# An S4 convolution and a Strassen FFN on one core: the first phase by pairs of row blocks

## The chip, the core and the metric

The kernel runs on one core of a Trainium2 chip. The metric is the device time in microseconds of one execution, the median of three runs. TensorE is PE (its weight loads PEld), VectorE DVE, ScalarE ACT, GpSimd POOL; SP is the engine whose queue issues nearly all transfers.

## What is computed

`x` has 4 batches of 1024 rows of 2048, float32: 32 row blocks of 128 rows, eight of one batch.

```python
mod = (silu(c) @ wmod).reshape(4, 6, 1, 2048)        # six sections, per batch
sa, ca, ga, sb, cb, gb = (mod[:, i] for i in range(6))
ga, gb = (sign(g) * max(abs(g), 0.25) for g in (ga, gb))
h = layernorm(x) * (1 + ca) + sa
x = x + ga * (causal_conv(h, K) + D * h)             # K: one S4 filter of 2048 taps, from Lambda, p, q, B, Ct, step
h = layernorm(x) * (1 + cb) + sb
x = x + gb * (h @ W.T + bias + low_rank_update(h))   # 16 adapters of rank 16, weighted sum
```

The convolution runs along the 2048 elements of a row, so it is a product with one triangular Toeplitz matrix of 2048 x 2048.

## The kernel before

Start. The filter is worked out (`s4`, `toeplitz`) and laid out as three 128-row tables `kf[f]`, each as a float16 high and low part. At the same time the sections 1 and 0 of the modulation (`ca`, `sa`) are formed: 16 steps each, a step loads 1 MB of `wmod` (`mod_load`, L312) and runs its matmuls (`mod_mm`, L317). `X0` says at which steps the first two blocks of x are loaded.

First phase, row block by row block (`r` from 0 to 31). `stats` (L493) takes mean and variance, `normalize` (L508) writes (x - mean) * rstd to a tile `n` on DVE. `conv_prep` (L522) works in four pieces of four 128-column chunks: four transposes on PE into PSUM (L535), four ACT instructions with scale `ca` and bias `sa` into `t` (L538), sums of neighbouring chunks (`sm`, L544), and the split of chunks and sums into a float16 high part (ACT copy, L546) and a low part (DVE subtraction, L547). `conv_mm` (L550) makes a row block's product in two halves `q`, each from three families of matmuls (L567); a family multiplies high by high, high by low and low by high. Family 0 works on the sums; ACT copies its result to `qs` (L580); family 2 gives the odd chunks with `qs` (L584), family 1 adds to family 0's PSUM and gives the even ones. The gate is multiplied in (L586, L593) and x is added with a running sum (L594). `conv_post` (L607) stores `y` to a scratch tensor `x1d`, takes the variance by an ACT Square that writes its elements over x, and keeps mean and rstd for the second layer norm in `ln2`.

Blocks 0 and 1 start before their gate is known (section 2 is formed meanwhile): `conv_late` (L598) gates them afterwards.

Between matmuls stand the generator `tick` and a list `PLAN`, one string for each of the 10 ticks of a row block: S is a step of fill, N a piece of the next block's preparation, T the statistics of the block after it, F its normalizing, P the block before's `conv_post`, L a step of the second phase's `left`. Fill (`rest`, L863) starts at block R0 = 3: it prepares the low-rank factors (`prep_lora`, L380), merges them into W in eight rounds (`merge`, L424, matmuls `lps` L443) and stores the merged weights as float16 pairs to `wcd`; every second step is one of sections 4, 3 and 5 of the modulation. The order on each engine is fixed when the program is built; it is mainly the text's, with single instructions pulled ahead where their operands are free.

Second phase. `left` (L636) loads two blocks of `x1d`, normalizes, transposes, modulates (256 wide, L655) and builds the seven left operands of a Strassen product, which it stores to `lfd` and keeps; `ffn_unit` (L692) multiplies them with the seven weights (L703), adds gate and bias to the residual (L721 to L728) and stores. It runs over all 16 units for the first half of the output columns and again for the second. The weights are loaded in `ORDER` = 0, 4, 5, 1, 6, 2, 3: weight 0 has a pool of its own, the next two (`XW`) reuse the four x tiles, the rest the space that the first phase leaves.

Of the kernel before, what the change touches and what calls it, by code (L numbers as in the profile page):

```python
# [34 lines left out]
class Net:  # L35
# [28 lines left out]
    def rstd(self, pool, var, out, n, name, scale=1.0):  # L64

        v = self.nc.vector
        ve = pool.tile([P, n], F32, tag=name + "_v", name=name + "_v")
        t = pool.tile([P, n], F32, tag=name + "_t", name=name + "_t")
        v.tensor_scalar(ve, var, 0.25 * scale, 0.25e-5, MUL, ADD)
        self.nc.scalar.activation(t, ve, AF.Sqrt)  # L70
        v.reciprocal(out, t)
        v.scalar_tensor_tensor(t, ve, out, t, MUL, ADD)
        v.reciprocal(out, t)

# [263 lines left out]
    def mod_gate(self, pool, name, bias=None):  # L338
# [10 lines left out]
        if bias is not None:  # L349
            bt = pool.tile([P, 512], F32, tag="mg2", name="mg2")  # L350
            for q in range(4):
                nc.sync.dma_start(out=bt[32 * q : 32 * q + 32], in_=bias[ds(512 * q, 512)].partition_broadcast(32))
            v.tensor_tensor(bt, bt, g, MUL)
            outs.append(bt)
# [138 lines left out]
    def stats(self, pl, x, tag):  # L493
        v = self.nc.vector
        st = pl["sm"].tile([P, 4, 6], F32, tag="st" + tag, name="st" + tag)
        for q in range(4):
            v.bn_stats(st[:, q], x[:, ds(512 * q, 512)])  # L497
        mv = pl["sm"].tile([P, 2], F32, tag="mv" + tag, name="mv" + tag)
        v.bn_aggr(mv, st)
        rs = pl["sm"].tile([P, 1], F32, tag="rs" + tag, name="rs" + tag)  # L500
        self.rstd(pl["sm"], mv[:, 1:2], rs, 1, "r" + tag)
        if tag in ACTNORM:
            mb = pl["sm"].tile([P, 1], F32, tag="mb" + tag, name="mb" + tag)
            v.scalar_tensor_tensor(mb, mv[:, 0:1], -1.0, rs, MUL, MUL)
            return mb, rs
        return mv, rs

    def normalize(self, pl, x, st, tag):  # L508
        n = pl["n"].tile([P, D], F32, tag="n", name="n" + tag)
        m, rs = st  # L510
        if tag in ACTNORM:
            self.nc.scalar.activation(n, x, AF.Identity, bias=m, scale=rs)
        else:
            self.nc.vector.tensor_scalar(n, x, m[:, 0:1], rs, SUB, MUL)
        return n

    def conv_load(self, pl, r):
        x = pl["x"].tile([P, D], F32, tag=f"x{r % 4}", name="x")
        self.nc.sync.dma_start(out=x, in_=self.io["x"][ds(P * r, P), :])
        return x  # L520

    def conv_prep(self, pl, r, x, st, out):  # L522
        nc, v = self.nc, self.nc.vector
        b = r // 8
        n = self.normalize(pl, x, st, "1")
        yield

        hc = [pl["h"].tile([P, NC, P], F16, tag=f"hc{x}", name=f"hc{x}") for x in range(2)]
        hs = [pl["h"].tile([P, HC, P], F16, tag=f"hs{x}", name=f"hs{x}") for x in range(2)]
        out[r] = hc, hs  # L530
        for c0 in range(0, NC, 4):
            tp = self.tps.tile([P, 4, P], F32, tag="t", name="tp")
            t = pl["t"].tile([P, 4, P], F32, tag="t", name="t")
            for k in range(4):
                nc.tensor.transpose(tp[:, k], n[:, ds(P * (c0 + k), P)], self.ident)  # L535
            for k in range(4):
                c = c0 + k
                nc.scalar.activation(  # L538
                    t[:, k], tp[:, k], AF.Identity,
                    bias=self.sa[:, c, b : b + 1], scale=self.ca[:, c, b : b + 1],  # L540
                )
            tv = t.rearrange("p (i e) n -> p i e n", e=2)
            sm = pl["t"].tile([P, 2, P], F32, tag="sm", name="sm")
            v.tensor_tensor(sm, tv[:, :, 0, :], tv[:, :, 1, :], ADD)  # L544
            for (hi, lo), src, sl in ((hc, t, slice(c0, c0 + 4)), (hs, sm, slice(c0 // 2, c0 // 2 + 2))):
                nc.scalar.copy(hi[:, sl], src)  # L546
                v.tensor_tensor(lo[:, sl], src, hi[:, sl], SUB)  # L547
            yield

    def conv_mm(self, pl, hs, x, tick, early):  # L550
        nc, v = self.nc, self.nc.vector
        hc, hs = hs
        y = pl["y"].tile([P, D], F32, tag="y", name="y")
        yv = y.rearrange("p (j e t) -> p j e t", e=2, t=P)
        if not early:
            gv = self.gat.rearrange("p (j e t) -> p j e t", e=2, t=P)
        sums = pl["sm"].tile([P, 2], F32, tag="sums", name="sums")

        def family(ps, f, q, first):
            pf = ps.rearrange("p j t -> p (j t)")  # L560
            last = 4 * q + 3
            for i in range(last + 1):
                o = P * max(0, i - 4 * q)
                k0 = P * max(0, 4 * q - i)
                for x, z in ((0, 0), (0, 1), (1, 0)):
                    h = hs[x][:, i] if f == 0 else hc[x][:, 2 * i + 2 - f]
                    nc.tensor.matmul(  # L567
                        pf[:, o:512], h, self.kf[f][z][:, ds(k0, 512 - o)],
# [6 lines left out]
        for q in range(2):  # L575
            jj = slice(4 * q, 4 * q + 4)
            pa = self.acc.tile([P, 4, P], F32, tag="a", name="ya")
            family(pa, 0, q, True)
            qs = pl["t"].tile([P, 4, P], F32, tag="qs", name="qs")
            nc.scalar.copy(qs, pa)  # L580
            tick()
            pb = self.acc.tile([P, 4, P], F32, tag="a", name="yb")
            family(pb, 2, q, True)
            v.tensor_tensor(yv[:, jj, 1, :], pb, qs, ADD)  # L584
            if not early:
                v.tensor_tensor(yv[:, jj, 1, :], yv[:, jj, 1, :], gv[:, jj, 1, :], MUL)  # L586
            tick()
            family(pa, 1, q, False)
            sl = ds(1024 * q, 1024)
            if early:  # L590
                nc.scalar.copy(yv[:, jj, 0, :], pa)
            else:
                v.tensor_tensor(yv[:, jj, 0, :], pa, gv[:, jj, 0, :], MUL)  # L593
                v.scalar_tensor_tensor(y[:, sl], y[:, sl], 1.0, x[:, sl], MUL, ADD, accum_out=sums[:, q : q + 1])  # L594
            tick()
        return y, sums

    def conv_late(self, x, y, sums):  # L598

        v = self.nc.vector  # L600
        for q in range(2):
            sl = ds(1024 * q, 1024)
            v.tensor_tensor(y[:, sl], y[:, sl], self.gat[:, sl], MUL)
            v.scalar_tensor_tensor(y[:, sl], y[:, sl], 1.0, x[:, sl], MUL, ADD, accum_out=sums[:, q : q + 1])
# [87 lines left out]
    def ffn_unit(self, pl, u, q, lf, wc, tick):  # L692
# [25 lines left out]
        for r, h in ((0, 0), (1, 1), (0, 1), (1, 0)):  # L718
            x = pl["o"].tile([P, 512], F32, tag="o", name="xo")
            nc.sync.dma_start(out=x, in_=at(self.x1d[2 * u : 2 * u + 2].rearrange("r p d -> (r p) d"), r, h))  # L720
            v.tensor_tensor(x, x, self.gbias[:, h], ADD)  # L721
# [39 lines left out]
ACTNORM = ""  # L761

MR = 2
ACC, TPS = 5, 2
PLAN = ("PNSL", "NL", "NSL", "NTL", "SL", "SL", "SL", "SL", "FSL", "SSL")
LPLAN = ("LL", "LL", "LL", "LL", "L", "0", "")
R0 = 3
WM, WMS = 3, 3
X0 = (21, 27)
LEFT0 = 30  # L770
# [12 lines left out]
def net(ctx: ExitStack, tc: tile.TileContext, io):  # L783
# [5 lines left out]
    k.ln2 = k.const("ln2", [P, 32, 2])  # L789
    k.lfd = k.dram.tile([NU, 7, P, HC, 2, P], F16, tag="lfd", name="lfd")  # L790
# [55 lines left out]
    xs, hs = {}, {}  # L846
    sts = {}
    n = 0
    for sec in (1, 0):
        for _ in section(sec, (wms, wmp)):  # L850
# [3 lines left out]
            if n in X0:  # L854
                r = X0.index(n)
                xs[r] = k.conv_load(pl, r)
                sts[r] = k.stats(pl, xs[r], "1")
            n += 1
    xs[2] = k.conv_load(pl, 2)
    st.close()  # L860
    for name, bufs in (("h", 2), ("n", 1), ("t", 2), ("y", 2), ("g", 1)):
# [19 lines left out]
    XW = {ORDER[1]: (0, 1), ORDER[2]: (2, 3)}  # L881

    def load_w(q, i):

        wc[i] = []
        for j in range(2):
            if i in XW:
                w = pl["x"].tile([P, D], F32, tag=f"x{XW[i][j]}", name=f"w{i}").bitcast(F16)
            else:
                w = pr["w" if i == ORDER[0] else "v"].tile([P, 2 * D], F16, tag=f"w{i}{j}", name=f"w{i}")  # L890
# [4 lines left out]
    def early():  # L895
        right.close()
        for name, bufs in (("w", 1), ("l", 8), ("t", 1), ("s", 1), ("x2", 1)):
            pr[name] = pool(p2, "p2" + name, bufs, "right")
        load_w(0, ORDER[0])
# [7 lines left out]
    def step():  # L907
        if r >= R0 and "w" not in pr and next(fill, 0) == 0:
            early()

    def prep(r):
        return k.conv_prep(pl, r, xs[r], sts.pop(r), hs)

    def load(r):
        xs[r] = k.conv_load(pl, r)

    def stats(r):
        sts[r] = k.stats(pl, xs[r], "1")

    sec = section(2, (wmp,))  # L920
    take(prep(0), 9)
    take(prep(1), 9)
    stats(2)
    take(sec, 16)
    load(3)
    ys = {0: k.conv_mm(pl, hs.pop(0), xs[0], lambda: None, True)}
    take(prep(2), 9)
    stats(3)
    ys[1] = k.conv_mm(pl, hs.pop(1), xs[1], lambda: None, True)
    nxt = prep(3)  # L930
    take(nxt, 1)
    take(sec, 1)
    k.gat = k.gate_tile(pl["g"], 0)
    for r in range(2):
        k.conv_late(xs[r], *ys[r])
        k.conv_post(pl, r, xs.pop(r), *ys[r])
    post = None
    for r in range(2, 32):
        if r + 2 < 32:
            load(r + 2)  # L940
        if r % 8 == 0:
            k.gat = k.gate_tile(pl["g"], r // 8)
        if r == 31:
            load_w(0, ORDER[1])
        if r == LEFT0:
            while "w" not in pr:
                step()
            lgen = next_left(0)
        plan = iter(PLAN)
        follow = []  # L950

        def tick():
            for a in next(plan):
                if a == "S":
                    step()
                elif a == "P" and post:
# [109 lines left out]
```

## Time and profile before

| | us |
|---|---|
| median of three runs | 2149.41 (2148.75 to 2149.71) |
| the profiled execution, its own time | 2148.25 |
| its span, first to last instruction | 2146.5 |
| busy PE, DVE, ACT, POOL | 2077.2, 1322.7, 926.2, 3.4 |
| first conv matmul, last one | 110.4, 924.8 |
| second phase's first matmul | 924.9 |

The mean granted clock of PE is 0.982; 483 MB are moved. A busy PE is no PE at its peak, since ends of matmuls are modelled: in the second phase matmuls of 512 columns start every 0.216 us and are shown as 0.379 each. The profile's lines of groups give the tile names, shapes and count, then busy time and mean, then the idle time of that engine before them with what ended it.

### The profile page before, as it was taken

The page shows a single profiled execution, that of the slowest core. Times are in us where ns is not written, and L with a number is a line of the kernel's source. Part 1 is how long each engine was busy: PE and PEld are TensorE (multiplying, and loading weights), DVE is VectorE, ACT ScalarE, POOL GpSimd, SP SyncE. Part 2 cuts the span into 40 slices and gives each one's busy share as a digit, 9 for nine tenths or more (in the row PEclk, how much of TensorE's full clock was granted, in tenths as well). Part 3 has the DMA queues.
Part 4 walks back from the last instruction along what each step waited for, and adds up shares of the span by engine and source line. Part 5 has one row for each costly group of instructions (what it writes and reads, how often), then busy time and mean ns, then how long its engine had stood idle before and what let it go on. Part 6 is the DMA issues. An engine that isn't in the chain of part 4 may idle for free.

```text
span 2146.5 us, 28399 instructions
## 1 busy us (share of the span) xinstructions
PE 2077.2 (97%) x11084; PEld 1021.9 (48%) x11084; DVE 1322.7 (62%) x2357; ACT 926.2 (43%) x1699; POOL 3.4 (0%) x12
## 2 busy tenths in 40 slices
PE   5698999999999999999999999999999999999998
PEld 1244545455455555654545545545444444444444
DVE  6549789988999998666565566565433323332323
ACT  1057667766677776655554455455200000000000
POOL 0000000000000000000000000000000000000000
PEclk8699999999999999999999999999999999999999
DMA  9988477767874553387465565565795545554542
GB/s 397 371 289 319 160 299 282 287 251 277 313 299 181 185 208 118 114 347 280 170 245 194 178 233 198 193 240 181 267 353 168 186 153 168 168 165 165 174 159 70
DMA packets 127137, 483.06 MB, mean 225 GB/s; under 512 B 13670, under 2 KB 13799, under 8 KB 96023
## 3 DMA queue, kind: packets, MB, share of 16 engines
q1 hardware_dynamic: 126464, 479.65, 61.7%
q8 instruction: 87, 1.43, 0.3%
q10 hardware_dynamic: 538, 1.59, 0.2%
q14 instruction: 48, 0.39, 0.1%
HBM read 325.89 MB, written 155.30 MB: 224 GB/s over the span
## 4 chain that ended last, share of the span: by engine, by line
PE 75%; DVE 11%; ACT 5%; DMA 2%; issue 1%; SPq 0%; POOL 0%; ACTq 0%; DVEq 0%
PE fZ L703 22%; PE fX L703 15%; PE fY L703 15%; PE ya L567 10%; PE yb L567 5%; PE tp L653 3%; PE lps L443 2%; PE modps L317 2%; ACT x L613 1%; PE tp L535 1%; ACT t L538 1%; DVE y L594 1%; DVE st L497 1%; DVE hc L547 1%; DVE wch L471 1%
## 5 line engine op out<-in xcount | busy, mean ns | idle before, releaser
L703 PEld LDWEIGHTS <-lf 128*128 128x128 f16 x5376 | 525.9, 98 | 620.8 <-issue 1.1
L703 PE MATMUL fZ<-w,lf 128*128 128x512 f16 x2304 | 513.6, 379 | 0.8 <-ACT p L711 0.8
L703 PE MATMUL fX<-w,lf 128*128 128x512 f16 x1536 | 342.8, 379 | 0.0
L703 PE MATMUL fY<-w,lf 128*128 128x512 f16 x1536 | 342.0, 379 | 0.0
L567 PEld LDWEIGHTS <-hc 128*128 128x128 f16 x2304 | 214.5, 98 | 202.0 <-issue 39.3
L721 DVE TENSOR_TENSOR xo<-xo,gb 128x512 f32<-128x512 f32 x128 | 87.8, 690 | 242.0 <-DMA xo<-x1d 229.6
L538 ACT ACTIVATE t<-tp,sa,ca 128x128 f32<-128x128 f32 x512 | 201.3, 473 | 13.2 <-DVE sa L376 5.1
L567 PE MATMUL ya<-kh,hs 128*128 128x512 f16 (+3 forms) x768 | 194.5, 328 | 0.7 <-DVE hs L547 0.7
L567 PE MATMUL ya<-kh,hc 128*128 128x512 f16 (+3 forms) x768 | 191.5, 327 | 3.2 <-ACT qs L580 3.2
L567 PE MATMUL yb<-kh,hc 128*128 128x512 f16 (+3 forms) x768 | 191.1, 326 | 0.0
L711 ACT COPY p<-fZ 128x512 f32<-128x512 f32 x64 | 37.2, 582 | 285.9 <-PE fZ L703 272.1
L711 ACT COPY p<-fX 128x512 f32<-128x512 f32 x32 | 18.7, 586 | 316.0 <-PE fX L703 240.9
L567 PEld LDWEIGHTS <-hs 128*128 128x128 f16 x1152 | 107.7, 98 | 98.4 <-issue 20.0
L655 ACT ACTIVATE gt<-tp,sb,cb 128x256 f32<-128x256 f32 x256 | 124.9, 575 | 60.9 <-PE tp L653 60.9
L317 PE MATMUL modps<-wm,sct 128*32 128x512 f32 x768 | 120.0, 687 | 28.4 <-DMA wm<-in_wmod 19.8
L567 PE MATMUL ya<-kl,hs 128*128 128x512 f16 (+3 forms) x384 | 126.1, 328 | 0.0
L567 PE MATMUL ya<-kl,hc 128*128 128x512 f16 (+3 forms) x384 | 125.5, 327 | 0.0
L567 PE MATMUL yb<-kl,hc 128*128 128x512 f16 (+3 forms) x384 | 125.4, 326 | 0.0
L726 DVE TENSOR_TENSOR fin<-fX,gb 128x512 f32<-128x512 f32 x32 | 22.1, 692 | 128.0 <-PE fX L703 127.9
L535 PE MATMUL tp<-ident,n 128*128 128x128 f32 x512 | 80.6, 282 | 15.1 <-ACT t L538 11.8
L547 DVE TENSOR_TENSOR hc<-t,hc 128x512 f16<-128x512 f32 x128 | 87.5, 683 | 5.5 <-ACT hc L546 5.5
L443 PE MATMUL lps<-lbh,lac 128*128 128x512 f16 x256 | 85.6, 382 | 1.3 <-ACT lbh L418 0.8
(241 smaller groups left out, 2212.8 us busy)
## 6 DMA issues: line engine op xcount, KB each, us to landing
wm<-in_wmod SPq DMA_DIRECT2D x96, 1024.0 KB, 6.3
lfd<-lf SPq DMA_DIRECT2D x112, 512.0 KB, 3.3
lf<-lfd SPq DMA_DIRECT2D x112, 512.0 KB, 3.9
x<-in_x SPq DMA_DIRECT2D x32, 1024.0 KB, 5.2
x1d<-y SPq DMA_DIRECT2D x32, 1024.0 KB, 5.7
x<-x1d SPq DMA_DIRECT2D x32, 1024.0 KB, 5.3
xo<-x1d SPq DMA_DIRECT2D x128, 256.0 KB, 3.9
out<-xo SPq DMA_DIRECT2D x128, 256.0 KB, 3.6
```

The costliest lines, as they stand in the source:

```text
L317: self.last = self.nc.tensor.matmul(self.modps[32 * g : 32 * g + 32, :], self.sct[:, j].rearrange("p r b -> p (r b)"), w[:, ds(512 * g, 512)],
L443: nc.tensor.matmul(ps, la[:, x, k, h], y[:, k, osl], start=(n == 0), stop=(n == 5))
L535: nc.tensor.transpose(tp[:, k], n[:, ds(P * (c0 + k), P)], self.ident)
L538: nc.scalar.activation(t[:, k], tp[:, k], AF.Identity, bias=self.sa[:, c, b : b + 1], scale=self.ca[:, c, b : b + 1],)
L547: v.tensor_tensor(lo[:, sl], src, hi[:, sl], SUB)
L567: nc.tensor.matmul(pf[:, o:512], h, self.kf[f][z][:, ds(k0, 512 - o)], start=first, stop=(i == last and (x, z) == (1, 0)), skip_group_chec ...
L653: nc.tensor.transpose(tp[:, c, r], xs[r][:, ds(P * (c0 + c), P)], self.ident)
L655: nc.scalar.activation(t[:, c0 + c], tp[:, c], AF.Identity, bias=self.sb[:, c0 + c, b : b + 1], scale=self.cb[:, c0 + c, b : b + 1],)
L703: nc.tensor.matmul(ps[name], lf[i][:, k, x, :], wc[i][k // 4][:, k % 4, y, :], start=(first and n == 0), stop=(n == 3 * HC - 1), skip_grou ...
L711: nc.scalar.copy(t, ps[name])
L721: v.tensor_tensor(x, x, self.gbias[:, h], ADD)
L726: v.tensor_tensor(t, cv, self.gbt[:, h], MUL)
```

## The change

The first phase goes by pairs `g` of row blocks. Both blocks' x are loaded together, and the statistics of both are finished together (`rstd` for two columns). Normalizing is an ACT instruction in place, over x itself; the residual is then rebuilt as x * std, without the mean, and the second phase adds the mean (`mv1`) where it adds the bias. A piece of the preparation covers four chunks of both blocks: eight transposes, four ACT instructions of 256, one sum of 512, and one high copy and one low subtraction of 1536 each (chunks and sums in one tile). `conv_mm` makes the first half of block 0, the first half of block 1, then the second halves. PLAN has 18 strings for a pair: O is the last piece of this pair's own preparation, N a piece of the next pair's, T its statistics, P the `conv_post` of the pair before's second block, Q that of this pair's first, S a step of fill and of `left`. Fill starts with pair 1. The tile `n`, the pool `w`, R0 and LEFT0 are gone, `mg2` shares a buffer; weights 0 and 4 take the x tiles.

```diff
-    def normalize(self, pl, x, st, tag):
-        n = pl["n"].tile([P, D], F32, tag="n", name="n" + tag)
...
-            self.nc.vector.tensor_scalar(n, x, m[:, 0:1], rs, SUB, MUL)
+    def stats(self, pl, g, xs):
...
+        rs = pl["sm"].tile([P, 2], F32, tag="rs", name="rs")
+        std = self.rstd(pl["sm"], mv[:, :, 1], rs, 2, "r1")
+        nb = pl["sm"].tile([P, 2], F32, tag="nb", name="nb")
+        v.scalar_tensor_tensor(nb, mv[:, :, 0], -1.0, rs, MUL, MUL)
+        return rs, nb, std
...
+    def conv_prep(self, pl, g, xs, st, out):
...
+        for r in range(2):
+            nc.scalar.activation(xs[r], xs[r], AF.Identity, bias=nb[:, r : r + 1], scale=rs[:, r : r + 1])
+        yield
+        out[g] = []
+        for k in range(4):
+            h = pl["h1" if k == 3 else "h2"].tile([P, 2, 6, 2, P], F16, tag=f"h{k}", name=f"h{k}")
+            t = pl["t"].tile([P, 6, 2, P], F32, tag="t", name="t")
+            out[g].append(h)
+            for i in range(2):
+                tp = self.tps.tile([P, 2, 2, P], F32, tag="t", name="tp")
+                for c in range(2):
+                    for r in range(2):
+                        nc.tensor.transpose(tp[:, c, r], xs[r][:, ds(P * (4 * k + 2 * i + c), P)], self.ident)
+                for c in range(2):
+                    d = 4 * k + 2 * i + c
+                    nc.scalar.activation(
+                        t[:, 2 * i + c], tp[:, c], AF.Identity,
+                        bias=self.sa[:, d, b : b + 1], scale=self.ca[:, d, b : b + 1],
+                    )
+            tv = t[:, 0:4].rearrange("p (i e) r n -> p i e r n", e=2)
+            v.tensor_tensor(t[:, 4:6], tv[:, :, 0], tv[:, :, 1], ADD)
+            nc.scalar.copy(h[:, 0], t)
+            v.tensor_tensor(h[:, 1], t, h[:, 0], SUB)
             yield
...
         for q in range(2):
+            for r in range(2):
+                y = ys[r]
...
+                family(pa, 0, q, r, True)
+                qs = pl["q"].tile([P, 4, P], F32, tag="qs", name="qs")
+                nc.scalar.copy(qs, pa)
+                tick()
...
+    def residual(self, x, y, std, sums, q):
+        sl = ds(1024 * q, 1024)
+        self.nc.vector.scalar_tensor_tensor(
+            y[:, sl], x[:, sl], std, y[:, sl], MUL, ADD, accum_out=sums[:, q : q + 1]
+        )
...
-            v.tensor_tensor(x, x, self.gbias[:, h], ADD)
+            m = self.mv1[:, 2 * u + r, 0:1]
+            v.scalar_tensor_tensor(x, x, m, self.gbias[:, h], ADD, ADD)
...
-PLAN = ("PNSL", "NL", "NSL", "NTL", "SL", "SL", "SL", "SL", "FSL", "SSL")
+PLAN = (
+    "POS", "S", "S", "S", "S", "S",
+    "TS", "S", "NS", "S", "S", "NS",
+    "QS", "NS", "S", "NS", "S", "S",
+)
...
-X0 = (21, 27)
-LEFT0 = 30
+X0 = 22
...
-    for name, bufs in (("h", 2), ("n", 1), ("t", 2), ("y", 2), ("g", 1)):
+    for name, bufs in (("h2", 2), ("h1", 1), ("t", 2), ("q", 1), ("y", 2), ("g", 1)):
...
-    XW = {ORDER[1]: (0, 1), ORDER[2]: (2, 3)}
+    XW = {ORDER[0]: (0, 1), ORDER[1]: (2, 3)}
...
+    for g in range(16):
+        if g:
+            if g + 1 < 16:
+                load(g + 1)
+            if g % 4 == 0:
+                k.gat = k.gate_tile(pl["g"], g // 4)
+        if g == 15:
+            while "l" not in pr:
                 step()
+            load_w(0, ORDER[0])
             lgen = next_left(0)
```

## The prediction

> **What bounds the kernel now.** I read the page's slices first, then a table of windows cut at the stage borders, then the waits of TensorE (PE) inside the first phase, then the groups of instructions with shapes kept apart.
>
> ```profile
> PE   5698999999999999999999999999999999999998
> DVE  6549789988999998666565566565433323332323
> ACT  1057667766677776655554455455200000000000
> PEclk8699999999999999999999999999999999999999
> ```
>
> A slice is 53.7 us. From slice 3 on PE is full to the end. DVE is nearly as full, but only to slice 14, ScalarE (ACT) never. A change that lightens DVE and ACT can therefore pay only where one of them, and not PE's own work, holds PE. The windows ask where that is (columns: window, length, busy time of PE, PEld, DVE, ACT, POOL, granted clock, DMA share, GB/s):
>
> ```profile
> 0.00:107.00 107.00, 68.67 (x326) 20.96 (x326) 62.11 (x165) 10.29 (x17) 1.91 (x10) 0.74 0.95 384
> 165.00:198.00 33.00, 32.05 (x192) 18.09 (x190) 31.32 (x71) 26.18 (x48) 0.00 (x0) 1.00 0.89 332
> 198.00:222.00 24.00, 16.13 (x75) 6.38 (x74) 23.11 (x59) 21.15 (x39) 1.06 (x1) 0.72 0.74 290
> 222.00:724.00 502.00, 494.03 (x3044) 257.33 (x3042) 447.58 (x909) 341.98 (x698) 0.00 (x0) 1.00 0.69 259
> 724.00:800.00 76.00, 72.55 (x454) 41.87 (x452) 73.35 (x167) 63.24 (x135) 0.38 (x1) 1.00 0.56 205
> 800.00:885.00 85.00, 84.17 (x538) 49.91 (x537) 69.62 (x158) 49.32 (x120) 0.00 (x0) 1.00 0.27 100
> ```
>
> Up to 107 us DMA sets the pace (0.95 of it busy: the modulation weights). From 222 to 885 PE idles 7.97 + 3.45 + 0.83 = 12.3 us, 12.6 with 885 to 925 (39.70 of 40). In 800 to 885, where no other work is mixed in, a row block takes 19.66 us (the copies qs at 826.20, 845.87, 865.53), and PE is busy 99% of it: no edit to DVE or ACT can shorten that. The one real hole is 198 to 222; on PE it reads
>
> ```profile
> 202.26 1.09 PE L535 MATMUL tp<-ident,n 128*128 128x128 f32 x8 [1.48 <-DVE n L514]
> 204.61 0.66 PE L535 MATMUL tp<-ident,n 128*128 128x128 f32 x4 [1.25 <-ACT t L538]
> 209.80 1.92 PE L317 MATMUL modps<-wm,sct 128*32 128x512 f32 x2 [1.86 <-DMA wm<-in_wmod]
> 212.53 0.58 PE L443 MATMUL lps<-lbh,lac 128*128 128x512 f16 x1 [0.82 <-ACT lbh L418]
> ```
>
> PE waits for normalizing, for modulation, for a weight tile, and then for the low-rank factors (`lbh`), whose preparation stands among the late gating of blocks 0 and 1 on a full DVE. Work in these 24 us at full rate: 26 modulation matmuls of 0.133, 16 transposes of 0.11, 7 lps and some 20 ya of 0.2: 11 us. So 13 us are lost.
>
> **The change, part by part.** Durations are from these rows:
>
> ```profile
> L538 ACT ACTIVATE t<-tp,sa,ca 128x128 f32<-128x128 f32 x512 | 201.3, 473 | 13.2 <-DVE sa L376 5.1 <-PE tp L535 3.2 <-DVE hc L547 3.1
> L655 ACT ACTIVATE gt<-tp,sb,cb 128x256 f32<-128x256 f32 x256 | 124.9, 575 | 60.9 <-PE tp L653 60.9
> L547 DVE TENSOR_TENSOR hc<-t,hc 128x512 f16<-128x512 f32 x128 | 87.5, 683 | 5.5 <-ACT hc L546 5.5
> L666 DVE TENSOR_TENSOR lf<-gt,lf 128x1024 f16<-128x1024 f32 x64 | 76.7, 1220 | 13.7 <-ACT lf L665 13.6
> L514 DVE TENSOR_SCALAR n<-x,mv,rs 128x2048 f32<-128x2048 f32 x32 | 42.9, 1341 | 4.2 <-PE tp L535 3.6
> L643 ACT ACTIVATE x<-x,ln 128x2048 f32<-128x2048 f32 x32 | 67.1, 2096 | 29.0 <-DMA x<-x1d 29.0
> ```
>
> Modulation: 512 ACT instructions of 128 become 256 of 256 wide, just the shape of L655 in the second phase: 201.3 to 124.9, ACT -76. The fp16 split: per pair of blocks eight copies of 512 and eight of 256 (82.1 + 54.8 us) become four of 1536. Copies of 512, 1024, 2048 take 0.64, 1.05, 1.89, so 1536 takes 1.47; 64 of them 94 us: ACT -43. Its subtraction: 0.683 at 512, 1.22 at 1024, so 1.76 at 1536; 64 are 112 against 87.5 + 53.2: DVE -28. The sums: 64 of 512 wide (44) for 128 of 256 (53.5): DVE -10. Normalizing leaves DVE (-42.9) for ACT, at 2.1 by L643: +67. Small statistics work for two blocks at once: some 1.0 us a pair for 0.68 a block, DVE -6, ACT -3. The residual keeps its form (1.22). Sums: DVE -87, ACT -55, PE nothing: transposes and matmuls keep number and size. In the second phase 128 additions at L721 (0.690) become the three-operand form, 0.744 at L445: DVE +7, hidden, as DVE is busy 324 of 535 us from 1000 to 1535; if uncovered, 7 us.
>
> What of this reaches PE:
> 1. **Idle of 222 to 925.** The windows 400 to 420, 540 to 560, 680 to 700 show DVE at 20.00, 20.00 and 19.70 of 20 and PE idle 2.45, 1.66, 2.75; with 3.45 in 724 to 800 (DVE 73 of 76) 10.3 of the 12.6 us stand where DVE is full. DVE loses 87 us of about 800, 2.2 in 20, so most of it closes: -8 (bounds 0 and -12.6). Next late there: nothing but PE.
> 2. **The hole.** DVE is busy 54.4 of 57 us from 165 to 222, three blocks are handled there, and a block gets 87/32 = 2.7 lighter: 8 us. The chain leaves DVE at 200 for ACT (lb, lbh) and returns at 212.5, so half comes through: -4. Bounds: -13, and +17 by the first rival. The row shows the granted clock at 0.72, and ya starting every 0.43 us from 212.9 to 218 that start every 0.22 later. The Trainium skill ("TensorE: Matmul & The Clock Gate", Part 1) says that the clock halves after an idle window of about 3.4 us and comes back after as long a busy one. By the row, shortening the hole by 4 is worth 4; by the rule the half-speed stretch (about 3.5 us of my 13) goes only if no idle window is left. I keep the row's: the hole does not close.
> 3. **The start.** Both x of pair 0 are loaded at step 22, and pair 1 is loaded before the end of the weight stream: one more MB in a saturated DMA, 2.5 us at 400 GB/s. The first usable split comes after 4 modulations (2.1), a sum (0.7) and a copy of 1.47 instead of 0.64: about +1. But both blocks' first halves follow at once, and the section-2 matmuls fill. Normalizing (4.2 on ACT, busy 10 of 107 us) is covered by the wait for `sa`. I take +2 (0 to +4).
> 4. **The opening of the second phase.** Weight 0 moves into x0 and x1, freed by pair 14 and so loaded in time; weight 4 now takes x2 and x3, and x3 is freed only by the last Square (929.2 to 931.1). So 11 MB instead of 9 follow that point (2.45 us each), one half of weight 4 first, whose matmuls start at 930.9 and need it 2.6 us later: +2 (-1 to +5). Left(0) gets 10 steps in one pair instead of two blocks, so its seven stores on SP no longer stand in front of the weights: that is the -1.
> 5. **New waits.** Load g+1 of x stands on SP behind the Square of the pair before: about 5 us into a pair, landing at 11; its statistics are called at tick 6 (12 to 14 us), normalizing at tick 8 (about 18). y of the second block waits for the store of the pair before: free at about 8 us, first needed at 9.9. Queued behind SP's wait are weight and WT loads; behind normalizing on ACT is qs, which PE needs within one family: 1.6 us in the first half, 4.2 in the second. The bound of no cost is if all fit; that of cost is 4.2 - 1.6 = 2.6 us a pair, 39 in all. All PE waits for qs from 225 to 925 now are 2.2 us, with the equally long Square on ACT in each block, and PLAN puts normalizing into the second half. I take +1. The Trainium skill ("Perfetto Trace Analysis", Optimizing Scalar/DVE Operations) speaks against this: engines that are not full but cause bubbles should get shorter instructions. By that rule ACT (342 of 502) should not get 1.47 and twice 2.1 us; it is right for ACT, and the +1 is its price, while DVE, the fuller engine, wants fewer.
>
> Sum: -8 - 4 + 2 + 2 + 1 = -7. The profiled execution took 2148.25, so 2141.25; the median of the runs is 1.16 above it: 2142.4. Differences under about 0.2% (4.3 us) can't be told from none here.
>
> **The rivals.**
> - *The low-rank work comes too early* (slower). Fill begins in pair 1 (block 2), not block 3, with a step in every tick. The first lps stands after one half family pair instead of after block 2 and half of block 3. If it keeps that place on PE, PE meets it at about 176 and waits to about 206 (lbh at 212.5 less the 4 to 6 saved): 30 us, against 13 lost now, +17, with the other terms +13: 2162. It decides from the point where less than some 17 us of pair 1's matmuls stand in front of the first lps. Against it: in the trace the loads of `la` and much later modulation matmuls are pulled ahead, so matmuls that are ready are moved too. For it: PE did stop at exactly this place.
> - *Handover between pairs* (slower): x or y late by 1 us in each of 15 pairs, +15 on the -7: 2157. Slack is about 2 us for y; against it is that in the fill stretch a pair takes 54 us, not 39.
> - *No change*: PE bound already, the idle stays with ACT's waits, the start and second phase eat the rest: 2149.
>
> **How the numbers follow.** Forecast 0.50 (own range 2134 to 2147); no change 0.18; early low-rank work 0.22; handover 0.10. Most of the forecast's chance is faster, its upper edge is the same: faster 0.49, same 0.19, slower 0.32. Low end: both idle terms at two thirds of their bounds, 2130. High end: the first rival with some of the second, 2166.
>
> **What would show it.** Right: DVE about 80 us and ACT 50 us less busy, PE busy time within a few us, 400 to 420 and its like without PE idle, still a hole with lps at its end near 200, a pair in the quiet stretch at 39.3 us. Wrong: idle PE before the first lps of over 17 us; waits of ya for qs of over 10 us; statistics waiting for x in each pair; a pair under 39.

## The result and the profile after

| | us | ratio to before (95%) |
|---|---|---|
| before, 4 runs | 2149.26 (2148.75 to 2149.71) | |
| changed, 4 runs | 2163.0 (2160.88 to 2165.06) | 1.0064 (1.0046 to 1.0081) |
| changed, profiled execution | 2160.88, span 2159.1 | |

The change made the kernel 0.64% slower, where 0.33% faster was forecast. The second phase took no part: from its first matmul to the end of the span it lasts 1220.65 us, before 1221.63. The first matmul of the second phase starts at 938.45, before at 924.87: all of the loss, 13.6 us, lies in the first phase. The page's totals and slices of the changed kernel:

```profile
PE 2070.2 (96%) x11084; PEld 1020.6 (47%) x11084; DVE 1273.2 (59%) x2037; ACT 912.2 (42%) x1267; POOL 2.7 (0%) x12
PE   5696999999999999999999999999999999999999
DVE  6537778887788877765666566565533323232323
```

DVE became lighter, as it was meant to (1322.7 before), and PE did not get fuller: the fourth slice (162 to 216 us) fell from 8 to 6. PE's idle time (span less busy) went from 69.3 to 88.9 us, +19.6; its busy sum fell by 7.0, a sum that depends on the granted clock and on how the ends of matmuls are modelled. The windows at the same borders (window, length, busy time of PE, PEld, DVE, ACT, POOL, granted clock, DMA share, GB/s):

```profile
165.00:198.00 33.00, 14.78 (x87) 7.06 (x86) 28.40 (x60) 25.99 (x34) 0.40 (x1) 0.74 0.95 375
198.00:222.00 24.00, 22.21 (x114) 11.27 (x114) 12.32 (x19) 11.04 (x11) 0.00 (x0) 0.86 0.24 88
222.00:724.00 502.00, 489.76 (x3013) 254.93 (x3010) 412.66 (x740) 335.17 (x459) 0.38 (x1) 1.00 0.69 252
724.00:800.00 76.00, 71.65 (x446) 41.14 (x447) 67.47 (x117) 53.20 (x71) 0.00 (x0) 1.00 0.58 215
800.00:885.00 85.00, 83.32 (x531) 49.46 (x529) 63.08 (x123) 53.47 (x72) 0.00 (x0) 1.00 0.27 100
```

The hole now comes one window earlier and is larger: in 165 to 222 PE now idles 20.0 us of 57, before 8.8. And from 222 to 925 it idles 19.0 us, before 12.6, although DVE is busy 412.66 us in the main window instead of 447.58. PE in the hole (start, length, engine, line, what; idle time before it and what ended it):

```profile
175.08 2.78 PE L322 MATMUL modps<-wm,sct 128*32 128x512 f32 x24
192.81 1.92 PE L322 MATMUL modps<-wm,sct 128*32 128x512 f32 x2 [14.95 <-DMA wm<-in_wmod]
199.79 0.58 PE L448 MATMUL lps<-lbh,lac 128*128 128x512 f16 x1 [5.06 <-ACT lbh L423]
```

The first modulation matmuls of the fill are reached at 175, PE then stands 15 us for a weight tile and 5 more for `lbh`, and the convolution matmuls of pair 1 are queued behind. The last of the two waits sets the length: `lbh` was there only at 199.8, so by the order on PE, which has the first `lps` next, PE would have stood to the same point without the wait for the weight tile. Before, the first `lps` came at 212.5: the fill now started earlier, and PE met it before its inputs were there.

Two transfers that SP issued at that time (start, length, queue, line, transfer), and the longest waits of SP's queue from 175 to 184 us (us in total, times, longest):

```profile
180.76 2.56 SPq L502 DMA_DIRECT2D x<-in_x  x2
183.41 1.47 SPq L317 DMA_DIRECT2D wm<-in_wmod  x3
```

```profile
SPq L618 <- DVE y L604: 5.1, 1, 5.1
SPq L618 <- DVE lsa_i L53: 4.2, 1, 4.2
```

The weight tile was issued at 183.41. In front of it on SP stood the two stores of `y` of blocks 0 and 1, which waited 5.1 and 4.2 us for DVE, and two loads of x, which waited 1.8 us for the Square that frees a tile.

The tile is that of the fill's fourth modulation step. In the program's text this is the fill's twelfth step, in the twelfth of pair 1's 18 ticks, with seven groups of `lps` in front; on PE its first matmul (the x2 at 192.81: each of these matmuls has two records) stands ahead of the first `lps`, and its other three run at 229.8. So the building of the program had pulled a matmul ahead, and PE stood for it.

### The profile page after: what moved, and what is told of

Its sections match the earlier page's. It is cut to its first block, busy times and chain, and to the rows that moved or that the text cites. A ratio compares the mean times of both kernels' runs of the same rounds, so it can differ in the third digit from the quotient of the medians.

```text
span 2159.1 us, 27722 instructions
## 1 busy us (share of the span) xinstructions
PE 2070.2 (96%) x11084; PEld 1020.6 (47%) x11084; DVE 1273.2 (59%) x2037; ACT 912.2 (42%) x1267; POOL 2.7 (0%) x12
## 4 chain that ended last, share of the span: by engine, by line
PE 62%; issue 25%; DVE 7%; DMA 3%; ACT 3%; SPq 0%; POOL 0%; POOLq 0%; DVEq 0%; ACTq 0%
PE fZ L712 23%; PE fX L712 15%; PE fY L712 15%; PE ya L569 3%; PE tp L662 3%; PE yb L569 2%; PE modps L322 1%; DVE h L549 1%; ACT x L622 1%; DVE y L604 1%; ACT h L548 1%; DMA xo<-x1d 1%; DVE s4wr L177 1%; DMA w<-wcd 1%; DVE st L513 1%
## 5 line engine op out<-in xcount | busy, mean ns | idle before, releaser
L569 PEld LDWEIGHTS <-h 128*128 128x128 f16 x3456 | 319.7, 98 | 317.1 <-issue 69.1
L569 PE MATMUL ya<-kh,h 128*128 128x512 f16 (+3 forms) x1536 | 380.5, 328 | 8.2 <-ACT qs L585 5.1
L569 PE MATMUL ya<-kl,h 128*128 128x512 f16 (+3 forms) x768 | 251.5, 328 | 0.0
L731 DVE SCALAR_TENSOR_TENSOR xo<-xo,mv,gb 128x512 f32<-128x512 f32 x128 | 95.2, 750 | 248.7 <-DMA xo<-x1d 236.7
L569 PE MATMUL yb<-kh,h 128*128 128x512 f16 (+3 forms) x768 | 192.2, 326 | 0.0
L542 ACT ACTIVATE t<-tp,sa,ca 128x256 f32<-128x256 f32 x256 | 126.2, 565 | 32.3 <-PE tp L539 23.4
L549 DVE TENSOR_TENSOR h<-t,h 128x1536 f16<-128x1536 f32 x64 | 112.2, 1754 | 28.2 <-ACT h L548 27.7
L569 PE MATMUL yb<-kl,h 128*128 128x512 f16 (+3 forms) x384 | 125.2, 326 | 0.0
L548 ACT CAST h<-t 128x1536 f16<-128x1536 f32 x64 | 94.1, 1470 | 26.2 <-DVE t L547 26.2
L675 DVE TENSOR_TENSOR lf<-gt,lf 128x1024 f16<-128x1024 f32 x64 | 76.7, 1220 | 18.3 <-ACT lf L674 18.2
L513 DVE BATCH_NORM_STATS2 st<-x 128x6 f32<-128x512 f32 x128 | 83.3, 681 | 5.1 <-DMA x<-in_x 5.1
```

The costliest lines, as they stand in the source:

```text
L513: v.bn_stats(st[:, q], xs[r][:, ds(512 * q, 512)])
L542: nc.scalar.activation(t[:, 2 * i + c], tp[:, c], AF.Identity, bias=self.sa[:, d, b : b + 1], scale=self.ca[:, d, b : b + 1],)
L548: nc.scalar.copy(h[:, 0], t)
L549: v.tensor_tensor(h[:, 1], t, h[:, 0], SUB)
L569: nc.tensor.matmul(pf[:, o:512], h[:, x], self.kf[f][z][:, ds(k0, 512 - o)], start=first, stop=(i == last and (x, z) == (1, 0)), skip_grou ...
L675: v.tensor_tensor(hl[:, :, 1, :], s, hl[:, :, 0, :], SUB)
```

## The experiments

Each line of time below is a median with its ratio to the kernel before, run on the same chip in the same batch. There were three batches, so versions of different batches are compared by their ratios. Where traces are compared, each is a single execution. Row blocks and pairs are counted from 0: pair 1 is blocks 2 and 3.

**The fill begins at pair 2.**

```diff
-        if g >= 1 and "l" not in pr and next(fill, 0) == 0:
+        if g >= 2 and "l" not in pr and next(fill, 0) == 0:
```

> The changed kernel with its fill (low-rank preparation, merges, sections 4, 3, 5) begun at pair 2 instead of pair 1. Theory A (the fill begins too early: on PE the first modulation and merge matmuls of the fill stand in front of all but one half block of pair 1, and wait there for a weight tile and for lbh): the hole of about 20 us near 178 to 200 shrinks to the size before or less, the time falls by 9 to 12, to 2151 to 2154. Rival B (the low-rank chain costs its wait wherever it stands): the hole moves behind pair 1 with its length, 2160 or more. Rival C (the loss is in the handover of x and y between pairs): no change, 2163.

2142.84 us (2137.64 to 2145.19), 0.9964 (0.9952 to 0.9976): 20 us better than the changed kernel, with all of the pair processing kept, and twice what theory A gave. The windows:

```profile
165.00:198.00 33.00, 33.00 (x198) 17.53 (x197) 30.76 (x60) 23.74 (x32) 0.00 (x0) 1.00 0.90 355
198.00:222.00 24.00, 23.22 (x153) 12.78 (x151) 17.33 (x40) 20.86 (x26) 1.13 (x1) 1.00 0.46 176
```

The hole is gone, 0.8 us of idle are left, and the clock is 1.00 throughout. The second phase begins at 917.94.

**The same question to the kernel before: fill at block 2, where the change put it, and at block 4.**

```diff
-R0 = 3
+R0 = 2
```

> The kernel before with its fill begun at block 2 instead of block 3, which is where the changed kernel begins it; nothing else. Theory A: the start of the fill is a cost by itself, without pairs: hole larger by 5 to 10, time 2154 to 2160. If the pairs' own order (loads of both x in front, halves in turn) makes the hole: 2148 to 2151.

```diff
-R0 = 3
+R0 = 4
```

> The kernel before with R0 = 4, so that the fill begins one row block later than it did (at row block 4, which is where pair 2 begins). Theory 'place': the late version of the changed kernel is faster than before only because its fill stands behind more convolution matmuls; then the kernel before has the same to gain: the 8.8 us of idle PE between 165 and 222 us and the half-speed stretch behind it go, some 8 to 11 us, 2139 to 2142. Rival 'pairs': the pairs themselves bring the 7 us, and the kernel before with the later fill stays within 3 us of 2149.5. A third outcome, that the fill then lacks room at the end of the first phase and closes with a queue of merges, gives 2152 or more.

With R0 = 2: 2159.7 us (2154.78 to 2163.26), 1.0046 (1.0033 to 1.0059). With R0 = 4: 2141.39 us (2140.1 to 2143.76), 0.9967 (0.9954 to 0.9979). The windows 165 to 198 and 198 to 222 of both, R0 = 2 first:

```profile
165.00:198.00 33.00, 18.28 (x107) 8.66 (x105) 27.78 (x66) 25.93 (x48) 0.79 (x1) 0.81 0.90 345
198.00:222.00 24.00, 18.31 (x71) 7.54 (x72) 15.45 (x31) 10.67 (x13) 0.00 (x0) 0.70 0.55 216
```

```profile
165.00:198.00 33.00, 31.87 (x191) 18.01 (x190) 31.18 (x71) 26.72 (x48) 0.00 (x0) 1.00 0.87 329
198.00:222.00 24.00, 23.46 (x158) 13.08 (x157) 24.00 (x63) 19.82 (x47) 0.43 (x1) 1.00 0.40 148
```

The kernel before makes the same hole when its fill starts at block 2 (20.4 us idle; 20.0 in the changed kernel). PE waits there 15.6 us for weight tiles and 2.5 for `lbh`, although x is loaded one block at a time: the two loads of a pair are not needed for it. With block 4 only 1.7 us of idle are left in these windows, but the end of the hole now lies behind them:

```profile
226.73 0.38 PE L443 MATMUL lps<-lbh,lac 128*128 128x512 f16 x1 [4.81 <-ACT lbh L418]
```

Up to block 4 the times fall into a table by place, not by kernel:

| fill begins at block | blocks one by one | pairs |
|---|---|---|
| 2 | 2159.7 (1.0046) | 2163.0 (1.0064), and 2161.73 (1.0061) in the batch of the 2159.7 |
| 3 | 2149.26 (the kernel before) | no such place |
| 4 | 2141.39 (0.9967) | 2142.84 (0.9964) |

At equal places the pairs can't be told from the blocks: the intervals of the ratios overlap.

**The low-rank preparation earlier, in pair 0.**

```diff
         def tick():
+            nt[0] += 1
+            if g == 0 and nt[0] == 4:
+                next(fill, None)
             for a in next(plan):
```

> The changed kernel with only the low-rank preparation pulled forward to the fourth tick of pair 0; merges and modulation steps stay where they are. If lbh ends the hole, the time falls by about 10 or more, to 2153 or less, and the first lps comes before 185. If the hole is ended by the modulation weight that waits on SP behind the loads of x (14.95 us of the 20 in the changed kernel), PE still stands there to about 193: only the 5 us for lbh go, 2158.

2162.13 us, 1.0057 (1.0043 to 1.007): nothing gained, against both expectations. The first steps of the preparation came 3 to 5 us earlier (ACT on `la` at 163.6 for 166.6, on `lb` at 178.1 for 182.9), but `lbh` was ready at 199.2 instead of 199.8: the earlier call did not bring its end forward, and PE waited for weight tiles before it (PE's waits of 160 to 225 us: engine, line, what for, us in total, times, longest):

```profile
PE modps L322 <- DMA wm<-in_wmod: 16.3, 3, 8.5
PE lps L448 <- ACT lbh L423: 2.7, 1, 2.7
```

**The load of pair 2 later.**

```diff
-            if g + 1 < 16:
+            if g + 1 < 16 and g != 1:
                 load(g + 1)
...
+            if g == 1 and nt[0] == 4:
+                load(2)
```

> The changed kernel with the two loads of x for pair 2 called at the fourth tick of pair 1 instead of at its start, so that the modulation weights need not stand behind them on SP. If the queue order on SP is what holds PE: the wait of modps for wm (14.95 us) goes, and PE goes on with pair 1; 2153 to 2156. If the low-rank chain is the true end of the hole: the wait is only renamed, PE stands until lbh at about 200, and the time stays at 2162 to 2164.

2161.73 us, 1.0061 (1.0049 to 1.0074). The order of instructions on PE, DVE, ACT and SP came out the same as the changed kernel's, row for row, so that this run is a repeat of it: it says nothing on SP's queue, and it gives the changed kernel a second measurement beside the other edits. Its trace also shows how much single executions differ: the same program's first convolution matmul starts at 114.95 here and at 109.95 in the trace of the changed kernel.

**The fill begins in the middle of pair 1.**

```diff
-                    step()
+                    if g > 1 or nt[0] > 9:
+                        step()
```

> The changed kernel with the fill begun in the middle of pair 1 (from its tenth tick on) instead of at its start or at pair 2. Theory 'place' with the price as a length: about half of the 39 us of pair 1's matmuls then stand in front of the fill's first ones, against an idle of some 20 us: most of the 20 us between the two known versions comes back, 2143 to 2149. Rival 'clash': the loss comes from the fill's ACT, DVE and DMA work meeting pair 1 and the load of pair 2 at all, whatever stands in front on PE: 2155 to 2162, since most of the low-rank preparation still falls into pair 1.

2161.3 us, 1.0058 (1.0045 to 1.007): in the range of "clash", but no proof of it, since the hole moved with the start:

```profile
198.00:222.00 24.00, 14.01 (x69) 5.58 (x68) 15.13 (x33) 15.76 (x15) 0.52 (x1) 0.72 0.76 299
```

165 to 198 is now full (33.00 of 33), and 10 us of idle at a clock of 0.72 stand in the next window, where PE meets 22 modulation matmuls at 200.8 and the first `lps` at 217.3, after 4.0 us of waiting for `lbh`. The price is not a length of matmuls in front, as the expectation had it: the last steps of the preparation moved back too (`lbh` cast from 215.4 on, in the changed kernel from 197.9 on; 5 us of this are a later start of this execution's convolution, 115.1 for 110.0). The hole is only half as long as the changed kernel's, so it is not the whole loss. From the first convolution matmul to the first of the second phase it takes 824.1 us here, 806.9 with the start at pair 2 and 828.5 in the changed kernel. Of the 17 us more than with pair 2, 9.2 are idle in the hole, 4.9 more idle behind 222 us (22.4 for 17.5); the rest fits the clock, which is 0.50 from 208 to 220.

**The preparation early, the fill's matmuls late.** This separates the order on PE from the preparation's load on the other engines.

```diff
+            if g == 1 and nt[0] == 1:
+                next(fill, None)
...
-        if g >= 1 and "l" not in pr and next(fill, 0) == 0:
+        if g >= 2 and "l" not in pr and next(fill, 0) == 0:
```

> The changed kernel with the fill cut in two: its first step (the low-rank preparation on DMA, ACT, DVE and POOL) stays at the start of pair 1, all other steps, with the modulation and low-rank matmuls, come from pair 2 on. Theory 'order on PE': the 20 us are lost because matmuls of the fill stand in PE's order ahead of ready convolution matmuls; with the preparation early and those matmuls late PE is not held: idle between 165 and 222 us below 3 us, 2140 to 2145. Rival 'clash': the preparation's transfers and ACT work, when they fall on pair 1 and the load of pair 2, slow the whole: 2155 to 2163.

2148.42 us (2144.37 to 2152.51), 0.9989 (0.9981 to 0.9997). ACT casts `lbh` from 203.3 on without a break, as in the changed kernel, but the first `lps` stands at 223.9:

```profile
165.00:198.00 33.00, 33.00 (x195) 17.34 (x194) 29.29 (x59) 25.74 (x37) 0.40 (x1) 1.00 0.96 380
198.00:222.00 24.00, 21.25 (x126) 10.86 (x124) 20.25 (x46) 19.99 (x21) 0.00 (x0) 0.94 0.61 229
```

Idle of 165 to 222 is 2.75 us, as "order on PE" has it; the time lies between the ranges of the two theories. By the ratios, the start at pair 2 brings 0.0100 (1.0064 to 0.9964; 21.5 us), and this version 0.0075 of it (16 us): three quarters come back with the preparation left early and only the steps behind it moved. These steps are PE's matmuls with their own loads and the merging on DVE and ACT; but DMA is as busy as in the changed kernel from 165 to 198 (0.96, there 0.95), and PE is full. The other 5 us go with the early preparation (the intervals of 0.9989 and 0.9964 are apart): 2.0 us more idle in the two windows and 3.7 more behind them (21.3 for 17.5, up to the second phase); PE's waits for `qs` from 225 to 925 are 8.6 us here and 2.8 with everything at pair 2, which fits long ACT instructions in the way of `qs`, but no run takes these apart.

**Later still.** The changed kernel with its fill from pair 3, and the kernel before with R0 = 5:

```diff
-        if g >= 1 and "l" not in pr and next(fill, 0) == 0:
+        if g >= 3 and "l" not in pr and next(fill, 0) == 0:
```

> The changed kernel with the fill begun at pair 3 (row block 6). Theory 'order on PE': at pair 2 nothing of the start is left to gain, the fill's last matmul moves from 729 to some 770 us, still far before the first FFN product at 918: 2141 to 2145, as with pair 2. Rival 'room': a shorter stretch for the fill packs it denser, and the waits within the phase (16 us with pair 2) grow: 2148 to 2155.

```diff
-R0 = 3
+R0 = 5
```

> The kernel before with R0 = 5. Theory 'order on PE': the hole is gone with R0 = 4 already, so nothing more comes: 2139 to 2144. If the start still mattered by length, another 5 to 10 us would come off: 2131 to 2136.

Pair 3: 2146.95 us (2142.23 to 2152.72), 0.9984 (0.9975 to 0.9994), some 4 us worse than pair 2, at the edge of what can be told (0.9964, 0.9952 to 0.9976). Idle from 222 to 910 us is 20.7 against 17.5: the denser fill has its price, in between what the two theories expected. R0 = 5: 2137.85 us (2136.68 to 2138.74), 0.9938 (0.9925 to 0.995), the fastest version run; 14.3 us idle in the same stretch, 18.6 with R0 = 4. The difference has the size of the 4.81 us for `lbh` that R0 = 4 had left; with R0 = 5 PE has no such wait. So with the hole wholly gone the blocks are ahead of the pairs: 0.9938 against 0.9964 at best, intervals just apart.

**The normalization on DVE again**, with the fill from pair 2 and from pair 3:

```diff
-            nc.scalar.activation(xs[r], xs[r], AF.Identity, bias=nb[:, r : r + 1], scale=rs[:, r : r + 1])
+            v.tensor_scalar(xs[r], xs[r], rs[:, r : r + 1], nb[:, r : r + 1], MUL, ADD)
```

> The changed kernel with the fill begun at pair 2, and the normalization in place done by DVE (tensor_scalar) instead of ACT. Theory 'ACT': the in-place normalization queues on ACT behind the modulation copies and Squares; on DVE the transposes' waits for x (6.6 us) nearly go, 2136 to 2140. Rival 'DVE': DVE is at 79% of the steady part, 32 more instructions of over 1 us each delay y and the halves of the outputs: 2144 to 2152.

> The changed kernel with the fill begun at pair 3 and the normalization in place on DVE. If both edits do what the single ones did (the normalization about -3 us against the version with pair 2, the later start nothing), 2138 to 2142. If DVE, which carries 80% and more in the steady part, meets the denser fill, 2145 or more.

Pair 2: 2140.12 us (2134.58 to 2142.45), 0.9959 (0.9945 to 0.9972), against 0.9964 with ACT: not told apart. PE's waits for the normalized x fall from 6.6 to 2.9 us. Pair 3: 2138.98 us (2136.56 to 2142.71), 0.9946 (0.9933 to 0.9958), against 0.9984 (0.9975 to 0.9994) with ACT in the same batch: 8 us, intervals apart. The two traces show only a part of this (the executions took 2142.71 and 2146.63 us; idle from 222 to 910 is 19.1 and 20.7), so where the rest of it lies is not shown. With DVE the pairs can no longer be told from the blocks with R0 = 5 (0.9946 and 0.9959 against 0.9938). In the window 400 to 600 us of the two versions from pair 2, ACT's first, then DVE's, DVE gets 12.5 us more to do and PE idles less, 0.8 us instead of 2.7:

```profile
400.00:600.00 200.00, 197.32 (x1215) 101.42 (x1217) 163.28 (x279) 135.43 (x183) 0.00 (x0) 1.00 0.75 278
400.00:600.00 200.00, 199.16 (x1234) 102.83 (x1232) 175.83 (x295) 121.57 (x179) 0.00 (x0) 1.00 0.75 279
```

**The loads of x issued by POOL**, with the fill from pair 2:

```diff
-            self.nc.sync.dma_start(out=x, in_=self.io["x"][ds(P * (2 * g + r), P), :])
+            self.nc.gpsimd.dma_start(out=x, in_=self.io["x"][ds(P * (2 * g + r), P), :])
```

> The changed kernel with the fill begun at pair 2, and the loads of x issued by POOL instead of SP. Theory 'queue': what is left of waits between 225 us and the end of the first phase (some 16 us, of which transposes waiting for the normalized x 6.6) comes from x loads that wait on SP for a Square and hold the y stores and weights behind them: POOL frees both, waits fall to 8 or less, 2134 to 2138. Rival 'chain': each x load is late because of the Square that frees its buffer, not because of its queue; nothing moves, 2141 to 2145.

2190.44 us (2185.1 to 2191.36), 1.0188 (1.0173 to 1.0202), 48 us worse than with SP, against both theories. In the trace DVE stops in front of the statistics, where it waits 2.5 us in all if SP issues the loads (DVE's waits of 225 to 918 us, the largest):

```profile
DVE st L513 <- DMA x<-in_x: 31.9, 12, 6.1
```

The loads still wait for the Squares (627.5 us in 24 waits on POOL), and land a median of 8.4 us after issue. From 165 us to the second phase PE idles 50.2 us, with SP 18.3. Why the statistics meet them so much less well was not settled.

## Why the prediction was wrong

The forecast failed at term 2, the hole, and at term 5, the new waits; the durations of the instructions were right, and term 1 had nearly its size by another cause than the one named. By the prediction's own steps:

- **Sizes of the instructions.** They were right. Groups of the changed kernel (out<-in, shapes, count, busy time, mean ns, idle before):

```profile
L542 ACT ACTIVATE t<-tp,sa,ca 128x256 f32<-128x256 f32 x256 | 126.2, 565 | 32.3 <-PE tp L539 23.4
L549 DVE TENSOR_TENSOR h<-t,h 128x1536 f16<-128x1536 f32 x64 | 112.2, 1754 | 28.2 <-ACT h L548 27.7
L548 ACT CAST h<-t 128x1536 f16<-128x1536 f32 x64 | 94.1, 1470 | 26.2 <-DVE t L547 26.2
```

  124.9, 112 and 94 us were foretold. Added up over all groups, ACT's rows fall by 60 us (1019 to 959; forecast 55) and DVE's by 75 (1443.2 to 1368.5; forecast 80, with the second phase's +7). The engines' totals, in which instructions that overlap count once, fall only by 14 and 50: part of what short instructions lose when they are joined had lain under their neighbours. So DVE's relief in term 1 was taken too large by a third (50 and the second phase's 7 for 87).
- **Term 2, the hole: -4 forecast, +11 idle measured (8.8 to 20.0).** The step that failed is "half comes through": it let a lighter DVE end the preparation sooner and took PE's place in the line as given. The preparation did end sooner (first `lps` at 199.8 for 212.5; the blocks with the same start have it at 204.7, so some 5 us of this are the pairs', as forecast, and 8 the earlier start). But PE met the fill at 175, since the change also moves the start of the fill one block ahead. This is the first rival, "the low-rank work comes too early". Its place held: it had PE meet the first `lps` at 176 and wait to 206; PE met the fill at 175 and was held until 199.8. That its time of 2162 is so near to the measured 2163.0 is in part luck: it had +17 for the hole and -7 for 222 to 925 (with all terms +14, not +13), measured are +11 and +6.5. Two details did not hold: the first 15 us are a wait for a weight tile, not for `lbh`; and "less than some 17 us of pair 1's matmuls in front" is no threshold of its own, since with the start half a pair later the loss stayed (2161.3). The kernel before with R0 = 2 shows that pairs are not needed for it.
- **Terms 1 and 5, the idle of 222 to 925: -8 and +1 forecast, together +6.5 measured (12.6 to 19.0).** PE's largest waits of 225 to 925, first in the kernel before, then in the changed one:

```profile
PE tp L535 <- ACT t L538: 7.0, 8, 1.8
PE ya L567 <- ACT qs L580: 2.2, 5, 1.0
```

```profile
PE tp L539 <- ACT x L528: 5.6, 5, 2.3
PE ya L569 <- ACT qs L585: 5.1, 8, 1.8
PE tp L539 <- ACT t L542: 2.9, 3, 1.8
PE ya L569 <- DVE y L589: 2.8, 1, 2.8
```

  Term 1 was nearly right in size. With the smaller waits, those for ACT's `t` fell from 7.3 to 3.6 us, and 2.5 us of waits for DVE are gone: about -6. In two of the three windows that the prediction names PE no longer idles, in the third 1.5 us for 2.75. But its reading that a full DVE makes this idle does not hold. The largest wait of the kernel before ends with ACT. In the windows 400 to 420 and 540 to 560 it makes up 1.8 of the 2.45 us and all of the 1.66, and ACT had worked for over five us in front of it without a gap, through a Square of 2.0 us and casts; of the waits for `t` over 1 us, only that at 691.0 had ACT itself standing for DVE before it (2.0 us). Moving the normalization back to DVE gave DVE some 40 us more (1271.9 to 1311.8), and lost no time with pair 2 and gained 8 us with pair 3; the waits for `t` are 4.7 us then, 4.0 without. So "next late there: nothing but PE" was wrong as well: most of what is left ends with ACT.
- **Term 5, the new waits: the step that failed is "I take +1".** They are 5.6 us for the normalized x, 2.9 more for `qs` (5.1 for 2.2) and 4.1 for `y` (2.8, and 1.3 at `lps`): about +12.6, where the bound named was 39. The 2.8 are for a `y` whose buffer came free late: SP stood 5.0 us for a store of merged weights, and the store of the earlier `y`, ready at 471.7, left at 475.1. The long ACT instructions were weighed against the Trainium skill ("Perfetto Trace Analysis", Optimizing Scalar/DVE Operations) and priced at +1; taking the 2.1 us normalization off ACT gained 8 us in one of two comparisons. That agrees with the page and says that +1 was too little, though no run broke an instruction up, which is what the page advises.
- **Term 3, the start: +2 forecast, about 0 measured**: the first convolution matmul starts at 109.95, before at 110.42.
- **Term 4, the opening of the second phase: +2 forecast, nothing measured there.** The last convolution matmul starts at 938.39, the first product at 938.45, and the whole phase is 1.0 us shorter.
- **The second rival**, handover between pairs, costs nothing in the quiet stretch: a pair takes 39.14 us (copies `qs` at 828.63 and 867.77), two blocks before took 2 x 19.66. In the fill stretch the 5.6 us for x and 2.8 for `y` under term 5 are of its kind, 8.4 us in six waits, where it had 15 us, 1 in each pair.

The chance given to the first rival, 0.22, was held down by the argument that ready matmuls are pulled ahead. The trace of before already spoke against it: PE stood in front of unready fill matmuls there too, for 1.86 us (a weight tile) and 0.82 (`lbh`). And the pulling ahead worked the other way: it put a modulation matmul whose tile was not there in front of pair 1's convolution. Of the signs of being wrong, idle PE before the first `lps` of over 17 us came (20.0); waits of `ya` for `qs` stayed under 10. One more sum is off, without weight: two thirds of both bounds give a low end of 2132, not 2130.

## What to carry to other kernels

When a change regroups loops, look first at what it does to the starting points of independent work that shares an in-order engine: here a start at block 2 instead of 4 cost 17 to 21 us in both kernels, and at equal starts the regrouping nothing that could be measured. An engine that is full where another idles is not shown to be the cause; see what ends each wait, and try the load the other way round. Compare the two versions with the shared filler work at the same place before crediting either, and then each at its best place: there the pairs were some 5 us behind the blocks (0.9964 and 0.9938), and with the normalization on DVE they could not be told apart.

## What was not expected

- A stall on PE costs more than its length, by the clock: after the 20 us of idle, `ya` matmuls of 512 columns start every 0.43 us from 200.2 to 201.0 in the changed kernel, for 0.22 at 167.5, and the full rate is back at 204.9; some 2 us are lost by it (an estimate from these rows). Short waits in a row do it too. In the kernel before no single wait from 198 to 212.5 is over 1.86 us, and yet the granted clock falls to a half (columns as in the windows above, the clock third from the end):

```profile
208.00:212.00 4.00, 1.92 (x2) 0.28 (x3) 3.84 (x10) 4.00 (x3) 0.00 (x0) 0.50 1.01 426
```

  With the preparation early and the matmuls late it is 0.50 from 220 to 224, behind waits of 1.88 and 0.99 us. The Trainium skill's clock gate ("TensorE: Matmul & The Clock Gate", Part 1), cited in the prediction, has the clock halve after an idle window of about 3.4 us. These traces agree with it after the long stall, but show that no single wait has to be that long; where 0.8 us of idle was left (the fill from pair 2), the clock stayed at 1.00.
- The framework's order can undo an edit: the later call of the load changed no row, and with the fill's start at pair 2 the preparation's first ACT instructions on `lb` still ran at 184.0, 182.9 with the start at pair 1. What moved was where the fill's matmuls stand on PE, and the end of the preparation.
- POOL as the issuer of 32 loads of 1 MB cost 48 us, though each issue took it a median of only 0.53 us.
